# Quarter swaps of convolution weights as transfers, interval products on two row tiles, and norms' roots by Newton steps

## The chip, the cores and the metric

The kernel runs on one core of a Trainium2 chip. The metric is the device time of one execution in microseconds, the median of several runs. TensorE (PE) multiplies matrices, VectorE is DVE, ScalarE is ACT, GpSimd is POOL; SyncE (SP) issues nearly all transfers here. A transfer is issued by a queue in program order, waits there for what it depends on, and lands some time later.

## The reference

The network takes x of shape (4, 32, 32, 16) in float32 through four residual layers, each `x = x + layer(groupnorm(x))` with eight groups of two channels. Layers 0, 1 and 3 are a position-dependent convolution:

```python
first = einsum('ijyx,byxc->bijc', M, inputs)
shifted = conv(inputs, K)      # 3x3, SAME; one kernel per position (i, j): 32*32*16 output channels
diff = relu(inputs - shifted)  # for every (i, j) an image of 32x32x16
second = einsum('ijyx,bijyxc->bijc', W, diff)
return first - second
```

So for each of 1024 positions (i, j), each of 16 channels and each of 4 images there is a whole 32x32 image of the 3x3 convolution (144 products each), then a minimum with zero, a weighting with W and a sum. Layer 2 treats the image's two sides as the ends of intervals: running maxima and minima, two steps of `max over k of sigmoid(f[i,k] Wf + r[k,j] Wr + b)`, and a last product with a sigmoid.

## The kernel before, in words

The four images are two groups of two (`NG`, `GB`). Six phases run one after the other: (group, convolution layer) for three layers. A phase has 8 chunks of 128 positions, a chunk 32 steps (channel f, image b), so there are 1536 steps. A step fills a pair of PSUM banks with 128 positions by 1024 pixels.

The convolution is a product over 144 rows, in float32r[...]. So weights and images are split in a high and a low part. Weights of four channels (`FU`) are a unit, and a unit serves 8 steps; there are 192 units. The first two (`PLAIN`) are used unsplit, in float32. All products use row tiles of 64 partitions: the two halves of the partition range work at once on the two halves of an image. Each half needs the other's weights too, so every split unit `parts` has two slots: slot 0 as computed, slot 1 with its halves of 64 partitions exchanged.

`prep_parts` (L220) is a generator that makes the units. Each step takes one `next` of it, so one unit's turn is spread over 8 steps. In it, `prep` (L208) subtracts the identity from the raw weights of the next unit on POOL; L203 takes the high bits on DVE; ACT scales and copies (L236, L240, L175 in `halve`); POOL subtracts (L237), adds W9 (L238) and WD (L241); then four casts on POOL (L243, L245) exchange quarters of 32 partitions between WU and WL. At last SP issues two transfers that fill slot 1 (L251) and the load of the raw weights two units on (L110 in `load_raw`). `parts` has three buffers, `raw` two.

In a step, `first_part` (L642) issues four pairs of products (ib with WL, ia with WU) and scales the sum on ACT (L663); `second_part` (L666) of the step before issues three pairs (iyz with WD, im9 with W9) and the product and sum on DVE (L680). Matmuls are on line L627.

All other work is laid between the steps by a second generator, `behind` (L733). What it yields is the number of steps to wait; `IDLE` or `CALM` means to wait until the yield of `prep_parts` in that step names this kind. In phase p it makes the inputs of phase p+1: the interval layer where due (L484), the norm (`group_norm`, L312), the copy to `xs` in DRAM and back into `raw` by 8 and 24 transfers (L381, L392), the split of both images (L274) and `place` (L290), which issues 12 transfers in one go. Further, it loads M in eight parts (L414) and issues the first terms (L418). In phase 0 it begins with `rest_of_start` (L869), which splits and places the first two images. W's rows are loaded at step 4 of each chunk (L116).

The schedule is written out by hand: the instructions of an engine and of SP's queue run in program order, and the order of the two generators in a step is: the next of `prep_parts`, the products, then `behind`.

```python
may = next(parts, (IDLE, CALM)) if n or at >= FIRST else (IDLE, CALM)
...
open_steps.append((step, first_part(step)))
if len(open_steps) > 1:
    second_part(*open_steps.pop(0))
wait -= 1
if wait <= 0 and (kind > 0 or kind in may):
    kind = wait = next(behind, 1 << 20)
```

Of the kernel before, what the change touches and what calls it, by code (L numbers as in the profile page):

```python
# [8 lines left out]
F32 = mybir.dt.float32  # L9
# [6 lines left out]
P = 128  # L16
# [28 lines left out]
def net_kernel(ctx: ExitStack, tc: tile.TileContext, x, xq, xi, convs, iv_w, iv_b, out):  # L45
# [162 lines left out]
    def prep(u, at=0, to=FU, eng=nc.gpsimd):  # L208
# [4 lines left out]
        for s in range(2 if u < PLAIN else 1):  # L213
# [3 lines left out]
                ALU.subtract,  # L217
            )

    def prep_parts():  # L220

        for u in range(PLAIN, n_chunks * NU):
            parts = wpool.tile([P, 2, 3, FU, P], F32R, tag="parts", bufs=AHEAD + 1, name=f"parts_{u}")
            W9 = wpool.tile([P, FU, P], F32R, tag="W9", bufs=AHEAD + 1, name=f"W9_{u}")
            units[u] = [parts[:, :, k] for k in range(3)] + [W9]
            src = raws.pop(u)
            w8 = src[:, 0].rearrange("p f k -> p (f k)")  # L230
            WU, WL, WD = (parts[:, 0, k].rearrange("p f k -> p (f k)") for k in range(3))
            high = upper(src[:, 0:1], 1, f"w{u}")[:, 0]
            yield (IDLE,)
            halve(W9, src[:, 1], low_w)
            yield ()
            nc.scalar.activation(WD, high, AF.Copy, scale=-EPS)  # L236
            nc.gpsimd.tensor_tensor(WL, w8, high, ALU.subtract)  # L237
            nc.gpsimd.tensor_tensor(W9, W9.bitcast(F32), src[:, 2], ALU.add)  # L238
            yield ()
            nc.scalar.copy(WU, high)  # L240
            nc.gpsimd.tensor_tensor(WD, WD.bitcast(F32), WL.bitcast(F32), ALU.add)  # L241
            for lo, hi in QUARTERS:
                nc.gpsimd.tensor_copy(WU[hi], WL[lo].bitcast(F32))  # L243
            for lo, hi in QUARTERS:
                nc.gpsimd.tensor_copy(WL[lo], high[hi])  # L245
            yield ()
            prep(u + 1)
            yield (IDLE,)
            yield (IDLE, CALM)
            for h in range(2):  # L250
                nc.sync.dma_start(  # L251
                    parts[64 * h : 64 * h + 64, 1].bitcast(F32),
                    parts[64 - 64 * h : 128 - 64 * h, 0].bitcast(F32),
                )
            load_raw(u + RAWS)
            yield (IDLE, CALM)
            yield (IDLE, CALM)

    def prep_plain(u, at=0, to=FU, eng=nc.gpsimd):
        if at == 0:  # L260
# [48 lines left out]
    def pair_view(ap):  # L309
        return ap.rearrange("p t (g s) -> p t g s", s=2)  # L310

    def group_norm(g, name, dst, gap):  # L312


        def sums(src):
            nc.vector.tensor_reduce(
                part[:, : GC // 2], src.rearrange("p t (g s) -> p g t s", s=2), axis=AX.XY, op=ALU.add
            )

        def totals(name):  # L320

            turned = work.tile([P, 32], F32, tag="turned", name=f"turned_{name}")
            nc.vector.transpose(turned, part)
            by_quarter = work.tile([32, 4], F32, tag="by_quarter", name=f"by_quarter_{name}")
            for q in range(4):
                nc.vector.tensor_reduce(
                    by_quarter[:, q : q + 1], turned[32 * q : 32 * q + 32], axis=AX.X, op=ALU.add
                )
            yield gap
            total = work.tile([P, 32], F32, tag="total", name=f"total_{name}")  # L330
            for q in range(4):
                nc.vector.tensor_reduce(
                    total[32 * q : 32 * q + 32, 0:1], by_quarter, axis=AX.X, op=ALU.add
                )
            yield gap
            whole = work.tile([P, 32], F32, tag="whole", name=f"whole_{name}")
            nc.vector.transpose(whole, total[:, 0:1].to_broadcast([P, 32]))
            return whole[:, : GC // 2]

        sums(X[g])  # L340
        yield gap
        m = yield from totals(f"m{name}")
        mean = work.tile([P, GC // 2], F32, tag="mean", name=f"mean_{name}")
        nc.gpsimd.tensor_scalar_mul(mean, m, 1.0 / (2 * NP))
        xc = work.tile([P, NT, GC], F32, tag="xc", name=f"xc_{name}")
        nc.gpsimd.tensor_tensor(pair_view(xc), pair_view(X[g]), spread(mean), ALU.subtract)
        sq = work.tile([P, NT, GC], F32, tag="sq", name=f"sq_{name}")
        nc.gpsimd.tensor_tensor(sq, xc, xc, ALU.mult)
        yield 4
        sums(sq)  # L350
        yield gap
        yield IDLE
        nc.scalar.activation(spare, spare, AF.Sqrt)
        v = yield from totals(f"v{name}")
        yield 2
        yield IDLE
        rstd = work.tile([P, GC // 2], F32, tag="rstd", name=f"rstd_{name}")
        nc.scalar.activation(rstd, v, AF.Sqrt, bias=eps, scale=1.0 / (2 * NP))
        yield 2
        nc.vector.reciprocal(rstd, rstd)  # L360
        nc.gpsimd.tensor_tensor(pair_view(dst), pair_view(xc), spread(rstd), ALU.mult)
        yield 3

# [54 lines left out]
    def first_terms(layer, mt):  # L418


        sums = bank_pair(f"pf_{layer}")
        for g in range(NG):
            for pt in range(NT):
                for j in range(4):
                    nc.tensor.matmul(  # L425
                        sums[32 * j : 32 * j + 32, g, :256],
                        lhsT=xns[g][:, pt, :], rhs=mt[:, pt, j, :],
                        start=pt == 0, stop=pt == NT - 1, tile_position=(0, 32 * j),
                    )
        ft = work.tile([P, NG, NT * GC], F32, tag="fs", name=f"ft_{layer}")  # L430
        for g in range(NG):
            nc.vector.transpose(ft[:, g], sums[:, g, : NT * GC])
        yield 1
        for g in range(NG):
            nc.vector.tensor_tensor(
                X[g], X[g], ft[:, g].rearrange("p (t m) -> p t m", t=NT), ALU.add
            )
            yield 1
# [7 lines left out]
    def constants():  # L446
        nc.sync.dma_start(wv, iv_w)
        nc.sync.dma_start(bv, iv_b)
        mask2 = const.tile([P, GB], F32, name="mask2")
        nc.vector.tensor_reduce(  # L450
            mask2, ident.rearrange("p (s b c) -> p b s c", b=GB, c=C), axis=AX.XY, op=ALU.add
        )

        nc.gpsimd.tensor_scalar_mul(mask2[GC : 2 * GC], mask2[GC : 2 * GC], -1.0)
        yield 2

        def blocks(dst, k, mask, n, p0=0):
            p = dst.shape[0]
            nc.gpsimd.tensor_tensor(
                dst,  # L460
                wv[p0 : p0 + p, k, :].unsqueeze(1).to_broadcast([p, n, C]),
                mask[p0 : p0 + p].unsqueeze(2).to_broadcast([p, n, C]),
                ALU.mult,
            )

        nc.gpsimd.memset(rt, 0.0)
        yield 1


        for k, hidden, name in ((0, None, "f0"), (3, 2, "f1"), (6, 5, "f2")):  # L470
            n = 64 if hidden is None else 96
            t = const.tile([n, GB, C], F32, name=name)
            blocks(t[:64], k, mask2, GB)
            if hidden is not None:
                blocks(t[64:], hidden, mask2, GB, 64)
            iv[name] = t.rearrange("p k c -> p (k c)")
            yield 1
        for k, name in ((1, "r0"), (4, "r1")):
            t = const.tile([64, NQ * GB, C], F32, name=name)
            for q in range(NQ):  # L480
                blocks(t[:, q * GB : (q + 1) * GB, :], k, mask2, GB)
            iv[name] = t.rearrange("p k c -> p (k c)")
            yield 1
    def interval_layer(g):  # L484
# [37 lines left out]
        def running(dst, src):  # L522
# [16 lines left out]
            out=r[:R, :H, 1:], in_=table(one), pattern=[[-1, H], [1, H]], compare_op=ALU.is_ge,  # L539
            fill=0.0, base=0, channel_multiplier=0,  # L540
        )
        yield 5

        def left(name, wf):
# [9 lines left out]

        def right_side(name, wr):

            for k0 in range(0, T1, 11):
                j0 = k0 + 1
                ps = bank(f"ps_{name}{g}{k0}")
                n = T1 - j0  # L560
                nc.tensor.matmul(  # L561
                    ps[:, : 11 * n], lhsT=wr, rhs=r[:R, k0 : k0 + 11, j0:], start=True, stop=True
                )
                nc.scalar.copy(
                    rt[:, j0:, k0 : k0 + 11],
                    ps[:, : 11 * n].rearrange("p (k j) -> p j k", j=n),
                )
                yield 1

        def step(name, ftp, bias):  # L570
# [17 lines left out]
                last = t  # L588
                yield 6 if i < QI else 3
            yield IDLE  # L590
            nc.scalar.activation(spare, spare, AF.Sigmoid)
            yield 2
            yield IDLE
            nc.scalar.activation(s, s, AF.Sigmoid, bias=bias)
# [224 lines left out]
    nc.vector.tensor_copy(mean_own, ps[:, :1])  # L819
    nc.vector.tensor_scalar_sub(XQ, XQ, mean_own)  # L820
    s2 = const.tile([P, 1], F32, name="s2")
    squares = const.tile([P, 256], F32, name="squares")
    nc.vector.scalar_tensor_tensor(
        squares, XQ, 1.0, XQ, op0=ALU.mult, op1=ALU.mult, accum_out=s2
    )
# [154 lines left out]
```

## Time and profile before

| | |
|---|---|
| median of three runs | 2477.75 us (2477.5 to 2477.88) |
| the profiled execution | 2478.41 us, of which the span is 2476.7 us |
| granted clock of TensorE | 1.000 |
| PE busy | 2458.2 us, 99% of the span |
| DVE, ACT, POOL busy | 2087.3, 1878.4, 1579.7 us (84%, 76%, 64%) |
| transfers | 366.92 MB; SP's queue 53.0% of the 16 DMA engines' span |
| POOL's casts between quarters | 380 + 380, 231.1 + 231.6 us |
| ACT's table loads | five of 1283 ns |

The page gives one line for each group of instructions: line, engine, operation, output and inputs, shapes, count, then busy time in us, the mean of one in ns, and the idle time of the engine just before with what ended it. The lines on transfers give the count, the KB of one and the median us from issue to landing. The chain is followed back from the last instruction to what released it, and gives shares of the span.

### The profile page before, as it was taken

Reading aid. Unit: us, or ns where it says so; the run is one execution under the profiler, and the core shown is the slowest. Engines: PE = TensorE matmul, PEld = TensorE weight load, DVE = VectorE, ACT = ScalarE, POOL = GpSimd, SP = SyncE. Lnnn points to the kernel's source line nnn. Section 1 sums busy time; section 2 is a strip of 40 time slices with the busy share of each in tenths; the row PEclk is TensorE's granted clock in tenths of the full one; section 3 lists DMA queues with packets and bytes.
Section 4 is the critical chain, followed back from the end, with each engine's and each line's share of the span. In section 5 each row is a group of like instructions: output and inputs, shape, how many; then the busy total and the mean of one; then the engine's idle time right before and its main releaser. Section 6 shows DMA issues by size and latency. Waiting matters only on the chain.

```text
span 2476.7 us, 58058 instructions
## 1 busy us (share of the span) xinstructions
PE 2458.2 (99%) x21906; PEld 2090.1 (84%) x21906; DVE 2087.3 (84%) x3617; ACT 1878.4 (76%) x2181; POOL 1579.7 (64%) x1750
## 2 busy tenths in 40 slices
PE   8999999999999999999999999999999999999999
PEld 5999888888888888888888988888998888888887
DVE  9888878888888888778898988899889888788887
ACT  4778767787777778777777777787777787677776
POOL 4766655666565657555567777586878676555552
PEclk9999999999999999999999999999999999999999
DMA  6446754466454467644454545574455467554442
GB/s 198 138 137 182 203 155 135 124 182 164 133 143 135 135 168 198 186 116 134 136 145 127 142 124 140 146 196 125 126 138 144 127 181 195 154 148 137 137 137 54
DMA packets 97673, 366.92 MB, mean 148 GB/s; under 512 B 26480, under 2 KB 31472, under 8 KB 97392
## 3 DMA queue, kind: packets, MB, share of 16 engines
q1 hardware_dynamic: 96832, 362.79, 53.0%
q8 instruction: 172, 2.82, 0.5%
q14 instruction: 109, 0.89, 0.1%
q10 hardware_dynamic: 432, 0.39, 0.1%
q0 software_dynamic: 128, 0.02, 0.0%
HBM read 199.78 MB, written 1.02 MB: 81 GB/s over the span
## 4 chain that ended last, share of the span: by engine, by line
PE 94%; DVE 2%; issue 1%; DMA 1%; ACT 0%; SPq 0%; POOL 0%; ACTq 0%; DVEq 0%; POOLq 0%
PE pc L627 93%; DVE junk L680 1%; PE pf L425 1%; DMA raw<-in_g 1%; ACT pc L663 0%; DMA first<-in_g 0%; SPq L298 0%; DVE raw L846 0%; SPq L300 0%; PE ps_l L548 0%; PE ps_r L561 0%; DMA parts<-parts 0%; DVE tables L508 0%; DVE raw L854 0%; DMA ib<-first 0%
## 5 line engine op out<-in xcount | busy, mean ns | idle before, releaser
L680 DVE SCALAR_TENSOR_TENSOR junk<-pc,WT 128x1024 f32<-128x1024 f32 x1536 | 1879.5, 1224 | 359.1 <-PE pc L627 308.3
L663 ACT ACTIVATE pc<-pc 128x1024 f32<-128x1024 f32 x1520 | 1532.0, 1008 | 561.0 <-PE pc L627 535.8
L627 PE MATMUL pc<-ib,parts 64*128 64x512 f32 x6080 | 958.5, 388 | 4.1 <-DVE junk L680 3.4
L627 PE MATMUL pc<-iyz,parts 64*128 64x512 f32 x6080 | 955.5, 387 | 2.2 <-ACT pc L663 2.0
L627 PE MATMUL pc<-ia,parts 64*128 64x496 f32 x6080 | 933.5, 379 | 0.0
L627 PEld LDWEIGHTS pc<-ia,parts 64*128 64x128 f32 x6080 | 595.5, 184 | 100.8
L627 PEld LDWEIGHTS pc<-ib,parts 64*128 64x128 f32 x6080 | 591.5, 184 | 105.0 <-DVE junk L680 9.9
L627 PEld LDWEIGHTS pc<-iyz,parts 64*128 64x128 f32 x6080 | 592.5, 184 | 88.4 <-ACT pc L663 6.4
L627 PE MATMUL pc<-im,W 64*128 64x496 f32 x3072 | 611.5, 384 | 0.0
L237 POOL TENSOR_TENSOR parts<-raw,upper_w 128x512 fp32r<-128x512 f32 x190 | 248.5, 1308 | 500.2 <-DVE upper_w L203 434.8
L627 PEld LDWEIGHTS pc<-im,W 64*128 64x128 f32 x3072 | 303.0, 184 | 54.5 <-issue 3.2
L243 POOL CAST parts<-parts 32x512 fp32r<-32x512 f32 x380 | 231.1, 608 | 50.1 <-ACT parts L240 31.8
L238 POOL TENSOR_TENSOR W<-W,raw 128x512 fp32r<-128x512 f32 x190 | 247.6, 1303 | 1.8 <-ACT W L175 1.8
L241 POOL TENSOR_TENSOR parts<-parts 128x512 fp32r<-128x512 f32 x190 | 246.8, 1299 | 2.0 <-ACT parts L236 1.9
L245 POOL CAST parts<-upper_w 32x512 fp32r<-32x512 f32 x380 | 231.6, 609 | 22.8
L214 POOL TENSOR_TENSOR raw<-raw,ident 128x512 f32<-128x512 f32 x190 | 199.9, 1052 | 52.2 <-DMA raw<-in_g 28.7
L175 ACT ACTIVATE W<-raw,low_w 128x512 fp32r<-128x512 f32 x190 | 136.2, 717 | 0.1
L680 DVE DVE_READ_ACCUMULATOR junk<-pc,WT 128x1 f32 x1536 | 127.5, 83 | 0.0
L236 ACT ACTIVATE parts<-upper_w 128x512 fp32r<-128x512 f32 x190 | 118.8, 625 | 6.6 <-DVE upper_w L203 6.4
L240 ACT CAST parts<-upper_w 128x512 fp32r<-128x512 f32 x190 | 116.5, 613 | 0.0
L695 POOL TENSOR_SCALAR acc<-acc 128x32 f32<-128x32 f32 x40 | 16.4, 409 | 141.7 <-DVE junk L680 139.7
L203 DVE TENSOR_SCALAR upper_w<-raw 128x512 int32<-128x512 int32 x190 | 86.1, 453 | 1.2 <-POOL raw L214 0.9
(139 smaller groups left out, 479.4 us busy)
## 6 DMA issues: line engine op xcount, KB each, us to landing
raw<-in_g SPq DMA_DIRECT2D x190, 768.0 KB, 7.1
parts<-parts SPq DMA_DIRECT2D x380, 384.0 KB, 4.9
WT<-in_w SPq DMA_DIRECT2D x48, 512.0 KB, 4.6
MT<-in_mt SPq DMA_DIRECT2D x24, 512.0 KB, 7.4
raw<-xs SPq DMA_DIRECT2D x120, 71.8 KB, 2.9
ib<-temp SPq DMA_DIRECT2D x40, 128.0 KB, 2.6
ia<-temp SPq DMA_DIRECT2D x80, 62.0 KB, 3.4
ib<-first SPq DMA_DIRECT2D x8, 128.0 KB, 2.4
```

Of the source, the lines that this page charges most:

```text
L175: nc.scalar.activation(dst, src, AF.Copy, scale=mask[:, 1:2])
L214: eng.tensor_tensor(raws[u][:, s, at:to], raws[u][:, s, at:to], pick[s][:, f0 + at : f0 + to].unsqueeze(2).to_broadcast([P, to - at, P]), ...
L236: nc.scalar.activation(WD, high, AF.Copy, scale=-EPS)
L237: nc.gpsimd.tensor_tensor(WL, w8, high, ALU.subtract)
L238: nc.gpsimd.tensor_tensor(W9, W9.bitcast(F32), src[:, 2], ALU.add)
L240: nc.scalar.copy(WU, high)
L241: nc.gpsimd.tensor_tensor(WD, WD.bitcast(F32), WL.bitcast(F32), ALU.add)
L243: nc.gpsimd.tensor_copy(WU[hi], WL[lo].bitcast(F32))
L245: nc.gpsimd.tensor_copy(WL[lo], high[hi])
L627: nc.tensor.matmul(ps[:, h, at : at + n], lhsT=w[r], rhs=v[r] if n == NH else v[r][:, :n], start=first and k == 0, stop=k == len(pairs) - ...
L663: nc.scalar.activation(ps, ps, AF.Copy, scale=1.0 + EPS)
L680: nc.vector.scalar_tensor_tensor(junk, ps.rearrange("p h n -> p (h n)"), 0.0, chunks[n], op0=ALU.min, op1=ALU.mult, accum_out=accs[phase][ ...
```

## The change

- The turn of a unit is ordered anew. POOL's subtraction (WL) comes before its sum for W9, and that for WD last. The four casts between quarters go; instead SP issues two transfers WL to WU and later two from the high part to WL. The two transfers that fill slot 1 (`exchange`) are issued in the turn of the next unit. `load_raw` moves ahead of the quarter transfers. The kinds that the yields name change with it, the number of yields per unit stays eight. The high part has two buffers of its own.
- The right products of the interval layer are placed on two row tiles: the pooled table is copied to partitions 64 to 127 (`below`), the weights have both copies, and the three products go to one pair of banks, the first on the upper tile, the other two on the lower.
- The norms' reciprocal roots come from an integer first guess (two operations on DVE) and four Newton steps on POOL (16 small operations) instead of a root on ACT and a reciprocal on DVE. The table of the sigmoid is fetched once, behind the first terms of layer 0.
- `squares` in the start shares the buffer `junk`.

```diff
+    def exchange(parts):
+        if parts is not None:
+            for h in range(2):
+                nc.sync.dma_start(
+                    parts[64 * h : 64 * h + 64, 1].bitcast(F32),
+                    parts[64 - 64 * h : 128 - 64 * h, 0].bitcast(F32),
+                )
+
     def prep_parts():
+        swapped = None
         for u in range(PLAIN, n_chunks * NU):
...
-            high = upper(src[:, 0:1], 1, f"w{u}")[:, 0]
+            halve(W9, src[:, 1], low_w)
+            yield (CALM,)
+            high = work.tile([P, FU * P], F32, tag="high", bufs=2, name=f"high_{u}")
+            nc.vector.tensor_scalar(
+                high.bitcast(I32), w8.bitcast(I32), HIGH, None, op0=ALU.bitwise_and
+            )
+            exchange(swapped)
             yield (IDLE,)
-            halve(W9, src[:, 1], low_w)
-            yield ()
+            prep(u + 1)
             nc.scalar.activation(WD, high, AF.Copy, scale=-EPS)
             nc.gpsimd.tensor_tensor(WL, w8, high, ALU.subtract)
+            yield (CALM,)
+            nc.scalar.copy(WU, high)
             nc.gpsimd.tensor_tensor(W9, W9.bitcast(F32), src[:, 2], ALU.add)
-            yield ()
-            nc.scalar.copy(WU, high)
+            yield (CALM,)
             nc.gpsimd.tensor_tensor(WD, WD.bitcast(F32), WL.bitcast(F32), ALU.add)
-            for lo, hi in QUARTERS:
-                nc.gpsimd.tensor_copy(WU[hi], WL[lo].bitcast(F32))
-            for lo, hi in QUARTERS:
-                nc.gpsimd.tensor_copy(WL[lo], high[hi])
-            yield ()
-            prep(u + 1)
-            yield (IDLE,)
-            yield (IDLE, CALM)
-            for h in range(2):
-                nc.sync.dma_start(
-                    parts[64 * h : 64 * h + 64, 1].bitcast(F32),
-                    parts[64 - 64 * h : 128 - 64 * h, 0].bitcast(F32),
-                )
             load_raw(u + RAWS)
             yield (IDLE, CALM)
+            for lo, hi in QUARTERS:
+                nc.sync.dma_start(WU[hi].bitcast(F32), WL[lo].bitcast(F32))
             yield (IDLE, CALM)
+            yield (IDLE, CALM)
+            for lo, hi in QUARTERS:
+                nc.sync.dma_start(WL[lo].bitcast(F32), high[hi])
+            swapped = parts
+            yield (IDLE, CALM)
+        yield (IDLE, CALM)
+        exchange(swapped)
...
+    def inverse_root(v, name):
+        n = GC // 2
...
+        nc.gpsimd.tensor_scalar(a, v, 1.0 / (2 * NP), 1e-5, op0=ALU.mult, op1=ALU.add)
+        nc.vector.tensor_scalar(
+            t.bitcast(I32), a.bitcast(I32), 1, None, op0=ALU.logical_shift_right
+        )
+        nc.vector.tensor_scalar(
+            y.bitcast(I32), t.bitcast(I32), -1.0, float(0x5F3759DF), op0=ALU.mult, op1=ALU.add
+        )
+        nc.gpsimd.tensor_scalar_mul(a, a, -0.5)
+        for pause in (1, 1, IDLE, 2):
+            yield pause
+            nc.gpsimd.tensor_tensor(t, a, y, ALU.mult)
+            nc.gpsimd.tensor_tensor(t, t, y, ALU.mult)
+            nc.gpsimd.tensor_scalar(t, t, 1.5, None, op0=ALU.add)
+            nc.gpsimd.tensor_tensor(y, y, t, ALU.mult)
+        return y
...
-        nc.scalar.activation(spare, spare, AF.Sqrt)
         v = yield from totals(f"v{name}")
-        yield 2
-        yield IDLE
-        rstd = work.tile([P, GC // 2], F32, tag="rstd", name=f"rstd_{name}")
-        nc.scalar.activation(rstd, v, AF.Sqrt, bias=eps, scale=1.0 / (2 * NP))
-        yield 2
-        nc.vector.reciprocal(rstd, rstd)
+        rstd = yield from inverse_root(v, name)
...
+        if layer == 0:
+            nc.scalar.activation(spare, spare, AF.Sigmoid)
...
+        below = tables[R:, : T1 * T1].rearrange("p (i j) -> p i j", j=T1)
+        nc.gpsimd.tensor_copy(below, r[:R])
+        tops = (r[:R], below)
...
-            for k0 in range(0, T1, 11):
+            ps = bank_pair(f"ps_{name}{g}")
+            blocks = []
+            for k0, h, at in ((0, 0, 0), (11, 1, 0), (22, 1, 11 * (T1 - 12))):
                 j0 = k0 + 1
-                ps = bank(f"ps_{name}{g}{k0}")
                 n = T1 - j0
+                blocks.append((k0, j0, n, ps[:, h, at : at + 11 * n]))
                 nc.tensor.matmul(
-                    ps[:, : 11 * n], lhsT=wr, rhs=r[:R, k0 : k0 + 11, j0:], start=True, stop=True
+                    blocks[-1][3], lhsT=wr[R * h : R * h + R], rhs=tops[h][:, k0 : k0 + 11, j0:],
+                    start=True, stop=True,
                 )
+            for k0, j0, n, sums in blocks:
                 nc.scalar.copy(
...
             yield IDLE
-            nc.scalar.activation(spare, spare, AF.Sigmoid)
             yield 2
...
-    squares = const.tile([P, 256], F32, name="squares")
+    squares = work.tile([P, NP], F32, tag="junk", name="squares")[:, :256]
```

More of the change, by code (lines that the diff above doesn't have):

```diff
@@ L310, in pair_view @@
         return ap.rearrange("p t (g s) -> p t g s", s=2)
+    def inverse_root(v, name):
+        n = GC // 2
+        a, y, t = (
+            work.tile([P, n], F32, tag=tag, name=f"{tag}_{name}") for tag in ("root_a", "root_y", "root_t")
+        )
[5 more added lines that the diff above has]
+            y.bitcast(I32), t.bitcast(I32), -1.0, float(0x5F3759DF), op0=ALU.mult, op1=ALU.add
+        )
+        nc.gpsimd.tensor_scalar_mul(a, a, -0.5)
[6 more added lines that the diff above has]
+        return y
     def group_norm(g, name, dst, gap):
@@ L452, in constants @@
         )
-        nc.gpsimd.tensor_scalar_mul(mask2[GC : 2 * GC], mask2[GC : 2 * GC], -1.0)
+        for at in (GC, 3 * GC):
+            nc.gpsimd.tensor_scalar_mul(mask2[at : at + GC], mask2[at : at + GC], -1.0)
         yield 2
@@ L478, in constants @@
         for k, name in ((1, "r0"), (4, "r1")):
-            t = const.tile([64, NQ * GB, C], F32, name=name)
+            t = const.tile([P, NQ * GB, C], F32, name=name)
             for q in range(NQ):
@@ L555, in right_side @@
         def right_side(name, wr):
-            for k0 in range(0, T1, 11):
+            ps = bank_pair(f"ps_{name}{g}")
+            blocks = []
+            for k0, h, at in ((0, 0, 0), (11, 1, 0), (22, 1, 11 * (T1 - 12))):
                 j0 = k0 + 1
-                ps = bank(f"ps_{name}{g}{k0}")
                 n = T1 - j0
+                blocks.append((k0, j0, n, ps[:, h, at : at + 11 * n]))
                 nc.tensor.matmul(
-                    ps[:, : 11 * n], lhsT=wr, rhs=r[:R, k0 : k0 + 11, j0:], start=True, stop=True
+                    blocks[-1][3], lhsT=wr[R * h : R * h + R], rhs=tops[h][:, k0 : k0 + 11, j0:],
+                    start=True, stop=True,
                 )
+            for k0, j0, n, sums in blocks:
                 nc.scalar.copy(
-                    rt[:, j0:, k0 : k0 + 11],
-                    ps[:, : 11 * n].rearrange("p (k j) -> p j k", j=n),
+                    rt[:, j0:, k0 : k0 + 11], sums.rearrange("p (k j) -> p j k", j=n)
                 )
```

## The prediction, made before the changed kernel ran

> **What bounds the kernel now.** I read the page's shares first, then its chain, then the transfers, then the timeline of SP's queue at the start.
>
> ```profile
> PE 2458.2 (99%) x21906; PEld 2090.1 (84%) x21906; DVE 2087.3 (84%) x3617; ACT 1878.4 (76%) x2181; POOL 1579.7 (64%) x1750
> PE 94%; DVE 2%; issue 1%; DMA 1%; ACT 0%; SPq 0%; POOL 0%; ACTq 0%; DVEq 0%; POOLq 0%
> L243 POOL CAST parts<-parts 32x512 fp32r<-32x512 f32 x380 | 231.1, 608 | 50.1 <-ACT parts L240 31.8
> L245 POOL CAST parts<-upper_w 32x512 fp32r<-32x512 f32 x380 | 231.6, 609 | 22.8
> raw<-in_g SPq DMA_DIRECT2D x190, 768.0 KB, 7.1
> parts<-parts SPq DMA_DIRECT2D x380, 384.0 KB, 4.9
> ia<-temp SPq DMA_DIRECT2D x80, 62.0 KB, 3.4
> ```
>
> TensorE is the bound. A step is seven pairs of row-tiled matmuls, and steps follow at 1.567 us (median distance of the DVE products of L680); 1536 of them are 2407 us of a span of 2476.7. The rest is the start (step 20 gets going at 50.5 us), 3 x 7.1 us of first terms, some 9 us of interval matmuls and about 7.5 us of short stalls. POOL is at 64%: its four casts of 0.61 us per unit are beside the path, since a unit lasts 8 steps = 12.5 us and POOL spends 8.3 us on it. So little can be won; what counts is whether a unit's weights stay ahead of the matmuls.
>
> The start, from SP's timeline (start, length, line, transfer) and PE's:
>
> ```profile
> 24.77 3.33 SPq L298 DMA_DIRECT2D ia<-first  x4
> 28.15 2.03 SPq L300 DMA_DIRECT2D ib<-first  x2
> 30.23 2.50 SPq L298 DMA_DIRECT2D ia<-first  x4
> 32.77 1.29 SPq L300 DMA_DIRECT2D ib<-first  x2
> 34.16 1.19 SPq L251 DMA_DIRECT2D parts<-parts  x2
> 35.39 1.21 SPq L110 DMA_DIRECT2D raw<-in_g  x1
> 36.69 3.33 SPq L298 DMA_DIRECT2D ia<-first  x4
> ...
> 43.33 0.64 PE L627 MATMUL pc<-ib,parts 64*128 64x512 f32 x4
> ```
>
> SP issues in program order: place of image 0 (12 transfers, about 0.63 us each), the half swap of unit 2, the load of unit 4, place of image 1. Unit 2's swap landed at 39.8 and step 16, its first user, began at 43.3. The load issued at 35.39 landed at 45.45, and the four small ones issued behind it at 36.69 to 39.49 landed at 45.6 to 46.2: **what stands behind a load on this queue lands after it**. Also, the eighth transfer after a load is not issued before that load lands (here 45.47 after 45.45; again 1603.96 after 1603.94).
>
> **What the Trainium skill says.** "DMA: Bandwidth & Descriptors", section "Queues, rings and completion order": one SDMA engine takes descriptors in ring order, without a promise of order over all engines; the landings above show the order in practice. Its section "Anatomy of one DMA" (GpSimd's path) has a fixed cost of about 2.0 us; here a 62 KB copy from SBUF to SBUF with nothing ahead landed 2.0 us after issue on SP. "ScalarE: Activation LUTs", section "What ACT_TABLE_LOAD costs": 1283 ns; the trace has five loads of 1283 ns. "TensorEngine Tiling (Array Packing)", section "Key Properties": different tiles may work in parallel; here the two 64-row matmuls of a pair start 3 to 4 ns apart.
>
> **Part 1, the swaps.** Removed: four casts, 2.43 us of POOL per unit, hidden now. Added: four 64 KB transfers per unit and three waits in a row on SP: WU's quarter goes behind load_raw, WL's quarter waits for it to land, and the half swap, now issued in the next unit's turn, waits for that. Behind these waits stand, on SP, the next load of `raw`, WT, MT, and the convolution input's transfers; POOL's `prep` waits for the load, PE for the swap. Before, the swap waited once, for POOL.
>
> The chain per unit, from `high` on DVE = 0: POOL's two adds (1.30 each) free `raw` at 0.45 + 2.60 = 3.05; the load is issued 3.05 to 4.2 and lands at 7.7 (1.9 us before data moves and 2.7 us of data, as 611.09 - 608.41 shows behind a swap); WU's quarters are issued to 5.3 and land behind it, 8.0; WL's are issued 8.0 to 9.1 and land at 10.9; the swap is issued 10.9 to 12.0 and lands 5.6 us after its first issue (602.80 to 608.41), at 16.6. The unit's first matmul comes 14 steps after the step of `high`, at about 20.4. **Margin 3.8 us.** Before: `high` at 608.15, swap issued at 615.34, landed at 620.92, used 15 steps after; the trace's median margin is 8.9 us. So in quiet stretches nothing is lost, but the cushion shrinks by about 5 us, while the least margins before were 0.8 (unit 124), 1.1 (42), 1.2 (3, 157), 1.5 (18) and 2.2 us (74): just where `place` and the loads of `raw` from xs fill SP.
>
> Start. The yields put the half swap of unit 2 in step 12, behind place of image 1 in step 11; before it was in step 9. Place of image 0 ends at 34.1 as now; load of unit 4 issued to 35.3, lands at 40 to 41; WU's quarters behind it, 41; WL's issued 41 to 42.2; place of image 1 then takes 12 x 0.63 = 7.6 us, to 49.8; the swap is issued at 49.8 and lands at 55.4. Step 16 begins there, step 20 four steps (6.3 us) later at 61.5, against 50.5: **+11 us**. Unit 3's chain runs meanwhile and arrives at about 67, when step 24 wants it (67.9).
>
> Later phases. Place (7.6 us) falls between WU's and WL's quarters in phases 1 to 4. 2.7 us of it hides in the wait for the load (5.3 to 8.0), so the swap is 4.9 us late, 1.1 more than the margin; the second place meets a queue with no cushion and the limit of eight in flight (five go, then the load's landing at 24.2 must come, then seven more), so the swap lands at 37.2 where 34.0 is wanted, 3.2 more. About 4.5 us per pair in phases 1 and 2, 5.6 in 3 and 4 (a weight load in between), 7.5 in phase 0 where image 0's place falls between WL's quarters and the swap with only the 2 us landing to hide in: 28 in all. The blocks of 8 xs and 24 raw<-xs issues (0.48 us each, 15 us) fall over two units; spread at two per step, mostly into waits, they cost 1.3 in phases 0 to 2; in phases 3 and 4 they are issued four per step, and a swap stands behind most of them: about 7 each. 18 in all. MT's loads (1.8 us of data each) take 1 in phases 0 and 2. Sum **+47, I take 45**. From below: if the idle gaps hide more, 10; from above, with less slack than I count (the margins that this walk gives for the old order come out up to 2 us too large), 75.
>
> POOL's order (subtraction, W9, then WD) and the reused buffer for `squares` cost nothing: POOL has a third of its time free.
>
> **Part 2, right products.** Three fp32 products of 0.59, 0.39 and 0.19 us (352, 231, 110 columns, two passes each) are 1.17 us of PE, four times. On two row tiles the first runs beside the others: at best 0.58 saved each time, 0.29 if in-order issue lets only half overlap: 1.2 to 2.3 us, **I take 1.7**. The copy of `r` (like L534, 2.2 us) hides in the five steps that follow the select.
>
> **Part 3, roots.** Four table loads in phases 3 and 4 (1420, 1564, 1832, 1976) are each followed by a PE stall of 0.55 us; one load remains, behind the first terms at 339 us, where ACT is idle for 7 us. **-2.2 us.** Added: 18 POOL instructions per norm of about 0.25 us (as L344), 4.5 us, eight times; waits of the same length in steps (1+1+2 plus an idle one for 2+2 plus one). POOL's freed time covers it. DVE loses a reciprocal (0.25) and gains two small operations of about 0.17: nothing. Where DVE's copies and scans meet PE's short stalls can shift: 0, from -4 to +4.
>
> **Sum.** The profiled execution took 2478.4 (span 2476.7 and 1.7 around it), 0.7 over the median 2477.75. 2478.4 + 11 + 45 - 1.7 - 2.2 = 2530.5; against the median, 2530.
>
> **Rivals.** (a) Only the start pays: SP's gaps swallow place and xs, since SP waits anyway. For it: the old order came through with 0.8 us. Against: those margins were what was left of 9, and the new chain starts with 4. 2477.75 + 11 - 4 + (0 to 20) = 2485 to 2505. (b) **Faster**: the quarter transfers don't stay behind the load, so that the chain is some 3 us shorter and POOL's relief makes the weights earlier. It decides if unit 2's swap lands before 43.3, which asks for SP to reach it before image 1's place; the program order speaks against it. Then only the savings are left, 3.9 plus up to half of the 7.5 us of stalls: 2470. (c) The casts' removal is not what the transfers replace one for one: if SP falls behind for good (swap 10.9, load landed 19.3, WU 19.6, WL 22.5 and the next swap: 11.6 us against 12.5), every phase loses more, 2565 and above.
>
> **How the numbers follow.** The forecast 0.63, (a) 0.20, (b) 0.10, (c) 0.07. A measurement of this kernel tells about 0.2% (5 us) from no change; a start that costs 11 less the savings and some luck gives 0.05 for the same. Slower 0.85, same 0.05, faster 0.10. The range 2484 to 2565 leaves out (b) and most of (c); the forecast's own is 2505 to 2565.
>
> **What would show it.** The first `ib` matmul of unit 2 at about 55 instead of 43.3, waiting for parts<-parts; PE waits on parts<-parts of 1 to 7 us near the old 195 to 245, 505 to 570, 905 to 970, 1590 to 1625 and 2000 to 2040 us, each later by what was lost before it; SP's waits of L251 turning from POOL to the quarter transfers; POOL near 47% busy; two table loads. Wrong: step 16 at 43, or no PE wait on parts after 70 us.

## The result and the profile after

The changed kernel took 2627.18 us (median of four runs, 2625.03 to 2634.42) against 2477.82 before: 1.0608 times, 95% interval 1.059 to 1.0626. The direction was as forecast. The size was not: +149 us, where +52 was forecast and +87 was the end of the range. The profiled execution has a span of 2626.3 us, 149.6 more than before.

From the page after, in the order of the lines shown of before: busy times and shares, the granted clock of TensorE in 40 slices, the chain, the costliest POOL group by idle time, and the transfers.

```profile
PE 2523.8 (96%) x21906; PEld 2207.3 (84%) x21906; DVE 2088.0 (80%) x3625; ACT 1875.2 (71%) x2159; POOL 1145.7 (44%) x1137
...
PEclk9999999999999999999999999899999989999999
...
PE 70%; DMA 14%; SPq 5%; DVE 4%; issue 3%; POOL 2%; ACT 1%; DVEq 0%; ACTq 0%; POOLq 0%
...
L214 POOL TENSOR_TENSOR raw<-raw,ident 128x512 f32<-128x512 f32 x190 | 201.1, 1058 | 640.4 <-DMA raw<-in_g 441.5
...
raw<-in_g SPq DMA_DIRECT2D x190, 768.0 KB, 5.2
parts<-parts SPq DMA_DIRECT2D x380, 384.0 KB, 4.9
...
parts<-parts SPq DMA_DIRECT2D x380, 64.0 KB, 4.8
parts<-high SPq DMA_DIRECT2D x380, 64.0 KB, 2.0
```

POOL lost 434 us of work, as meant. But PE's share of the chain fell from 94 to 70%, and transfers and SP's queue have 19% of it. WU's quarters (64 KB, 4.8 us) wait behind the load; WL's (2.0 us) don't. More is moved, 416.82 MB instead of 366.92, but the two transfers that the chain had before did not slow down: the half swap still lands 4.9 us after issue in the median, and the load of `raw` after 5.2 instead of 7.1. PE is busy for 65.6 us more with the same 21906 matmuls, and two of its 40 clock slices fell below nine tenths. The waits of after say what PE and ACT waited for (waiter, released by: us in total, times, longest):

```profile
PEld pc L662 <- DMA parts<-parts: 92.1, 50, 9.0
PE pc L662 <- DMA parts<-parts: 72.3, 47, 8.5
...
ACT parts L250 <- DVE high L244: 34.6, 44, 4.7
PEld pc L662 <- ACT pc L698: 31.3, 61, 1.4
```

The first two were absent before, and they count the same waits on two rows of PE. Before, PE's weight loads waited for ACT 6.4 us in 11 waits.

The start, in the timeline of SP's queue and of PE after:

```profile
34.25 0.53 SPq L110 DMA_DIRECT2D raw<-in_g  x1
34.83 1.19 SPq L260 DMA_DIRECT2D parts<-parts  x2
39.34 1.14 SPq L264 DMA_DIRECT2D parts<-high  x2
40.57 2.45 SPq L309 DMA_DIRECT2D ia<-first  x4
43.07 1.29 SPq L311 DMA_DIRECT2D ib<-first  x2
44.40 2.49 SPq L309 DMA_DIRECT2D ia<-first  x4
46.94 1.29 SPq L311 DMA_DIRECT2D ib<-first  x2
48.27 1.24 SPq L223 DMA_DIRECT2D parts<-parts  x2
```

```profile
43.30 0.40 PE L662 MATMUL pc<-ib,parts 64*128 64x512 f32 x2
52.23 0.79 PE L662 MATMUL pc<-ib,parts 64*128 64x512 f32 x1 [8.54 <-DMA parts<-parts]
54.05 0.79 PE L662 MATMUL pc<-ib,parts 64*128 64x512 f32 x1 [1.02 <-DMA parts<-parts]
54.15 1.51 PE L662 MATMUL pc<-ia,parts 64*128 64x496 f32 x4
```

The half swap is issued behind the twelve transfers of place; its halves land at 52.2 and 54.0 (forecast 55.4), and PE stands for 9.6 us. Then four matmuls take 1.51 us, where four took 0.62 before. The trace's record of the granted clock is at 0.50 from 48.6 to 58.8 us, so it fell while PE still stood.

In a quiet stretch the chain runs as worked out. SP's timeline after, one unit from swap to swap:

```profile
834.72 1.14 SPq L223 DMA_DIRECT2D parts<-parts  x2
839.56 0.33 SPq L110 DMA_DIRECT2D raw<-in_g  x1
840.00 1.18 SPq L260 DMA_DIRECT2D parts<-parts  x2
844.58 1.14 SPq L264 DMA_DIRECT2D parts<-high  x2
847.15 2.18 SPq L223 DMA_DIRECT2D parts<-parts  x2
```

On POOL, the subtraction of the unit whose swap is the first of these:

```profile
824.20 1.30 POOL L251 TENSOR_TENSOR parts<-raw,high 128x512 fp32r<-128x512 f32 x1 [4.24 <-DVE high L244]
```

`high` ended at about 824.2, where the subtraction began; the swap issued at 834.72 landed at 840.22, 16.5 us after `high` began (16.6 forecast). The median margin, from the landing of a swap to its unit's first matmul, is 3.0 us (3.8 forecast).

To place the loss I took, for each of the 190 split units, the time from the last `im9` product before it to its first `ia` product, less the 0.665 us of a unit that doesn't wait. Before, these waits sum to 0.4 us; after, to 95.3, in 33 units:

| place | units | forecast | measured |
|---|---|---|---|
| start | 2 | 11 | 10.8 |
| place, phases 0 to 4 | 17, 18; 42, 43; 74, 75; 125, 126; 157, 158 | 28 | 30.5 |
| copies to xs and back | 14; 38, 39; 70, 71; 123; 155 | 18 | 39.6 |
| loads of M and W | 20, 22, 23, 46, 48, 80, 165, 167 | 1 to 2 | 9.3 |
| others | | 0 | 5.1 |

That leaves 54 us that are no waits for weights.

### The profile page after: what moved, and what is told of

Read it like the earlier page. It is cut to its first block, busy times and chain, and to the rows that moved or that the text cites. A ratio compares the mean times of both kernels' runs of the same rounds, so it can differ in the third digit from the quotient of the medians.

```text
span 2626.3 us, 59027 instructions
## 1 busy us (share of the span) xinstructions
PE 2523.8 (96%) x21906; PEld 2207.3 (84%) x21906; DVE 2088.0 (80%) x3625; ACT 1875.2 (71%) x2159; POOL 1145.7 (44%) x1137
## 2 busy tenths in 40 slices
DMA packets 134159, 416.82 MB, mean 159 GB/s; under 512 B 38640, under 2 KB 43632, under 8 KB 133872
## 4 chain that ended last, share of the span: by engine, by line
PE 70%; DMA 14%; SPq 5%; DVE 4%; issue 3%; POOL 2%; ACT 1%; DVEq 0%; ACTq 0%; POOLq 0%
PE pc L662 69%; DMA parts<-parts 9%; DVE junk L715 2%; DMA raw<-in_g 2%; DMA parts<-high 2%; SPq L419 1%; ACT pc L698 1%; PE pf L452 1%; SPq L309 1%; SPq L264 1%; POOL W L254 1%; SPq L223 1%; POOL parts L251 1%; SPq L311 1%; SPq L408 1%
## 5 line engine op out<-in xcount | busy, mean ns | idle before, releaser
L662 PE MATMUL pc<-ib,parts 64*128 64x512 f32 x6080 | 1041.4, 393 | 80.6 <-DMA parts<-parts 72.3
L662 PE MATMUL pc<-iyz,parts 64*128 64x512 f32 x6080 | 1023.1, 393 | 9.9 <-ACT pc L698 9.0
L662 PE MATMUL pc<-ia,parts 64*128 64x496 f32 x6080 | 1004.3, 384 | 0.0
L662 PEld LDWEIGHTS pc<-ib,parts 64*128 64x128 f32 x6080 | 665.1, 186 | 175.7 <-DMA parts<-parts 92.1
L662 PEld LDWEIGHTS pc<-ia,parts 64*128 64x128 f32 x6080 | 665.8, 187 | 72.6
L662 PE MATMUL pc<-im,W 64*128 64x496 f32 x3072 | 665.8, 387 | 0.0
L251 POOL TENSOR_TENSOR parts<-raw,high 128x512 fp32r<-128x512 f32 x190 | 247.1, 1301 | 383.7 <-DVE high L244 292.1
L254 POOL TENSOR_TENSOR W<-W,raw 128x512 fp32r<-128x512 f32 x190 | 247.2, 1301 | 0.1
L250 ACT ACTIVATE parts<-high 128x512 fp32r<-128x512 f32 x190 | 119.2, 627 | 40.0 <-DVE high L244 34.6
L253 ACT CAST parts<-high 128x512 fp32r<-128x512 f32 x190 | 115.9, 610 | 0.0
L730 POOL TENSOR_SCALAR acc<-acc 128x32 f32<-128x32 f32 x40 | 12.5, 312 | 214.7 <-DVE junk L715 210.1
L244 DVE TENSOR_SCALAR high<-raw 128x512 int32<-128x512 int32 x190 | 94.2, 496 | 0.2
```

The lines of the kernel that those rows point to most:

```text
L244: nc.vector.tensor_scalar(high.bitcast(I32), w8.bitcast(I32), HIGH, None, op0=ALU.bitwise_and)
L662: nc.tensor.matmul(ps[:, h, at : at + n], lhsT=w[r], rhs=v[r] if n == NH else v[r][:, :n], start=first and k == 0, stop=k == len(pairs) - ...
```

## The experiments

**What each part costs.** Theory A: part 1 makes the weights late, and TensorE's clock falls after longer waits. Theory B: the other parts carry a good share. The first kernel is the old one with the new `exchange` and `prep_parts` (and `squares` in `junk`'s buffer):

```diff
...
-            for lo, hi in QUARTERS:
-                nc.gpsimd.tensor_copy(WU[hi], WL[lo].bitcast(F32))
...
+            for lo, hi in QUARTERS:
+                nc.sync.dma_start(WU[hi].bitcast(F32), WL[lo].bitcast(F32))
...
```

> The kernel before with part 1 alone (quarter swaps as transfers, the order of POOL's work, the half swap in the next unit's turn); roots and right products as before. Theory A (the chain of three transfer waits on SP makes the weights late, and TensorE's clock drops to half after the longer waits): all of the 149 us come with it, and the savings of the other parts are missing, 2628 to 2635 us. Theory B (Newton's steps on POOL, or the products on two row tiles, carry a good part): below 2580 us.

Measured: 2626.02 us, ratio 1.0599 (1.0583 to 1.0614). Part 1 is the whole loss. The second has parts 2 and 3, with the old `prep_parts`; against the kernel before:

```diff
...
-        rstd = work.tile([P, GC // 2], F32, tag="rstd", name=f"rstd_{name}")
-        nc.scalar.activation(rstd, v, AF.Sqrt, bias=eps, scale=1.0 / (2 * NP))
...
+        rstd = yield from inverse_root(v, name)
...
```

> The changed kernel with part 1 undone: casts on POOL as before, roots by Newton steps and right products on two row tiles kept. Theory A: 3.9 us less than before (2.2 from table loads, 1.7 from the products), 2474 us, from 2470 to 2478. Theory B: over 2500 us.

Measured: 2483.94 us, ratio 1.0021 (1.0012 to 1.003): slower by 5, where 3.9 were to be saved. By units, the savings are there (0.5 us at each of four units with right products, 0.7 at two without a table load), but units 99, 131, 122 to 126 and 154 to 158 lose more. From the waits of this kernel between 1276 and 1290 us, at unit 99:

```profile
DVE upper_w L203 <- POOL raw L214: 2.0, 1, 2.0
PEld pc L651 <- DVE junk L704: 2.0, 2, 1.2
PE pc L651 <- DVE junk L704: 1.2, 2, 0.7
```

My reading: with the casts kept, Newton's steps stand ahead of `prep` on POOL, which began at 1280.72 behind steps from 1279.59 on; DVE stood 2.0 us for it before it could take the high bits, its products came late, and PE waited for a free bank. To tell whether it was the products, they were put into the old kernel alone:

```diff
...
-                    ps[:, : 11 * n], lhsT=wr, rhs=r[:R, k0 : k0 + 11, j0:], start=True, stop=True
+                    blocks[-1][3], lhsT=wr[R * h : R * h + R], rhs=tops[h][:, k0 : k0 + 11, j0:],
...
```

> The kernel before with the right products on two row tiles alone (casts, roots and tables as before). If Newton's steps on POOL made the kernel without part 1 slower (DVE waited 2 us for POOL's prep behind them), this one is 1 to 2 us faster than before, 2476 to 2478. If the copy of the pooled table or the row tiles made it, it is 3 to 6 us slower.

Measured: 2476.71 us, ratio 0.9992 (0.9983 to 1.0001). So the products don't slow it: it is 1.7 us under the runs of before beside it (2478.4), as expected, though the interval just touches no change. That leaves the roots; alone they were not run.

**What the chain waits for.** First, the half swap of unit 2 alone is issued in its own turn again:

```diff
             swapped = parts
+            if u == PLAIN:
+                exchange(parts)
+                swapped = None
```

> The changed kernel, but the half swap of unit 2 alone is issued in its own turn, right after WL's quarters, so ahead of place of image 1. Theory A: it is issued at about 42 and lands at 47.5 instead of 54.0; step 16 starts then; 7 us less, about 2620 us, a little more if the clock stays up. Theory C (the start is bound by image 1's place anyway, since step 20 waits for it): no more than 3 us less.

Measured: 2623.57 us, ratio 1.0593 (1.0576 to 1.0611). The 3.6 us less are within the intervals, so the time decides neither for 7 us nor for under 3. The trace tells more: unit 2's wait fell from 10.8 to 4.1, but unit 3 now waits 3.0, and each wait is followed by a stretch at half clock. Theory A was right about unit 2 and overlooked that the next unit's chain is behind as well.

Then the load of `raw` is issued behind the quarters:

```diff
-            load_raw(u + RAWS)
...
             swapped = parts
+            load_raw(u + RAWS)
```

> The changed kernel, with the load of raw issued after WL's quarters instead of ahead of WU's. Theory A with the wait behind the load as its main part: WU's quarters land at 4.9 us after high instead of 8, WL's at 8, the load at about 11, and the swap, now behind the load, at about 14.3 instead of 16.6; the margin grows by 2.3 us, most waits of PE under that size go, 2560 to 2595 us. Theory D (SP's time for place and the copies from xs sets the waits, wherever the load stands): within 10 us of 2627.

Measured: 2625.7 us, ratio 1.0598 (1.0582 to 1.0614). It came out on the side of theory D (SP's time for the other transfers sets the waits), with no gain that can be told. The load is then ahead of the swap instead of the quarters; the median margin is 3.4 us for 3.0, not 2.3 more.

Next, one of the chain's three waits on SP is taken out: WU's quarters are cast on POOL again.

```diff
+            for lo, hi in QUARTERS:
+                nc.gpsimd.tensor_copy(WU[hi], WL[lo].bitcast(F32))
             load_raw(u + RAWS)
             yield (IDLE, CALM)
-            for lo, hi in QUARTERS:
-                nc.sync.dma_start(WU[hi].bitcast(F32), WL[lo].bitcast(F32))
```

> The changed kernel, but WU's quarters are cast on POOL again (1.2 us per unit) and only WL's quarters are transfers, so one of the three waits of the chain is gone. Theory A: WL's quarters go at about 5.6 us after high and land at 7.7 to 8.7, the swap lands at 14.3 instead of 16.6 at the latest, and SP has 1.2 us of issues less per unit: waits fall by a half, with the clock 60 to 90 us less, 2540 to 2570. Rival (E4's lesson holds for all of the chain, its length doesn't matter): within 10 us of 2627.

Measured: 2585.89 us, ratio 1.0434 (1.0417 to 1.0451). The median margin rose to 5.9 us and the waits fell from 95 to 65, by a third where a half was expected, so the time missed its range of 2540 to 2570. The length of the chain does count: 41 us of 149 hang on this one wait and its two issues, which this kernel takes out together.

**What stands between the chain's steps.** Copies from xs, two per step in phases 3 and 4 too:

```diff
-            if layer < 2 or row % 2:
-                yield 1
+            yield 1
```

> The changed kernel; the copies raw<-xs of layer 2's phases are given out two per step, as in the other layers, instead of four per step. Theory D (the wait before a unit is the time that SP spends on other transfers between the steps of the chain, less the gaps in which SP waits anyway): PE's waits before units 123 and 155 (12.5 and 11.3 us) fall to about those of units 38 and 39 (5 us), 15 us less, about 22 with the clock, 2605 us. Theory E (the waits come from the amount of work per phase, not from its density): under 5 us less.

Measured: 2633.66 us (one run). Unit 123 waits 8.3 instead of 12.5 and unit 155 7.5 instead of 11.3, but units 126, 127, 158 and 159 now wait 6.6, 4.3, 4.0 and 3.0: the sum stays at 95.8. By the time it is theory E (the amount of work counts, not how densely it is issued); by the waits, the spread copies reach into the units that place comes to and leave them no cushion.

The same transfers and place from POOL's queue:

```diff
...
-                nc.sync.dma_start(
+                nc.gpsimd.dma_start(
                     inner[:, h, r], xt[g][GC * r : GC * (r + 1), :, HW * h : HW * h + WP]
...
```

> The changed kernel; the copies to and from xs and, after the start, place are issued from POOL's queue instead of SP's. Theory D: the chain of SP is left with weights, W and M; waits before units 14, 17, 18, 38 to 43, 70 to 75, 123 to 126 and 154 to 158 are gone (some 72 of 95 us), and TensorE's clock stays up there; what is left is the start (13 us), M and W (10) and the small items: 2500 to 2520 us. Rival: POOL's own time for each issue makes the subtractions late by as much: over 2560 us.

Measured: 2622.51 us, ratio 1.0571 (1.0546 to 1.0597). The rival came true, and the kernel doesn't settle theory D. POOL's timeline there, ahead of unit 14:

```profile
190.96 4.70 POOL L408 DMA_DIRECT2D xs<-xt  x8 [2.92 <-DVE xt L402]
195.67 1.05 POOL L214 TENSOR_TENSOR raw<-raw,ident 128x512 f32<-128x512 f32 x1
196.66 1.30 POOL L251 TENSOR_TENSOR parts<-raw,high 128x512 fp32r<-128x512 f32 x1
197.92 1.30 POOL L254 TENSOR_TENSOR W<-W,raw 128x512 fp32r<-128x512 f32 x1
```

These eight issues cost POOL 0.59 us each, in front of the sum (L254) that frees `raw`. Therefore the transfers were left out altogether:

```diff
-        for r in range(ROWS):
+        for r in range(0):
...
-            for h in range(2):
+            for h in range(0):
                 off = tap // 3 * WP + tap % 3
```

> The changed kernel without the 8 copies to xs and the 24 copies from xs into raw per convolution input (left out: later phases work on the first phase's image). Theory D: the waits before units 14, 15, 38, 39, 70, 71, 123 and 155 (40 us) go, with them some six stretches at half clock (about 2 us each), 50 to 60 us less: 2565 to 2580 us. Theory F (each cycle of the chain is late by itself in these phases, through M's and W's loads or POOL): waits of several us stay there, over 2600 us.

Measured: 2574.12 us, ratio 1.0386 (1.0365 to 1.0407). The waits before 14, 38, 39, 70, 71, 123 and 155 are gone; the sum is 59.1. Without place in later layers as well:

```diff
-            yield from place(g, b, temp)
+            yield from place(g, b, temp) if layer == 0 else (1,)
```

> As before it (no copies to and from xs) and without place in the layers after the first (left out: the split images of later layers; place of phase 0 and of the start stays). Theory D: of the waits, the start (10.8 us), phase 0's place (up to 7.7) and M and W (up to 9) stay; the clock falls to half only around those: 2510 to 2535 us. Theory F: over 2570 us.

Measured: 2532.34 us, ratio 1.0217 (1.0197 to 1.0238). Waits sum to 27.0, of which 10.9 are the start and 7.2 phase 0's place; two stretches at half clock are left of 15. The control is the kernel before with the same transfers left out:

> The kernel before without the same transfers (no copies to and from xs, no place after the first layer): the control. Every theory: nothing of them is on the path there, 2472 to 2479 us.

Measured: 2475.41 us, ratio 0.9987 (0.9978 to 0.9996). The same 32 and 24 transfers per phase cost the old order 3 us and the new one 95. Theory D holds, and theory F (the chain is late by itself) falls: what stands between the chain's steps makes most of the loss. These kernels take away the transfers' bytes together with their place in SP's queue; that it is the place in the queue is read from the timelines and from the swap's median landing time, 4.8 us without them and 4.9 with them.

**What a wait of PE costs.** Eight waits put into the old kernel, one per chunk:

```diff
...
+                if at == 14 and n in HOLDS:
+                    hold_pe(phase, t, steps[at - 2], HOLDS[n])
...
+        for k in range(n):
+            nc.gpsimd.tensor_tensor(hold, ident, ident, ALU.mult)
+        nc.tensor.matmul(
+            bank(f"ps_hold_{phase}_{t}")[:, :1], lhsT=ident, rhs=hold[:, 0:1], start=True, stop=True
+        )
...
```

> The kernel before with eight deliberate waits of PE in quiet chunks of phases 1 and 2: a small product waits for a chain of 0, 2, 4, 6, 8, 11, 14 and 20 POOL operations that starts when DVE ends the sum two steps back. About 0.3 us per operation and 1 to 2 us at the base, so waits of 1 to 8 us. Theory A on the clock: waits under 2 us cost themselves alone; those over about 3.5 us are followed by a stretch of 3.4 us or a multiple at half clock, which costs 1 to 3 us more. Rival (the excess over the waits has another source, such as slower operands while transfers run): each wait costs its own length and the clock record stays at one.

Measured: 2545.46 us (one run). By the clock record and the start of the next unit:

| PE idle, us | 1.87 | 2.83 | 3.77 | 4.82 | 5.69 | 7.12 | 8.55 | 11.40 |
|---|---|---|---|---|---|---|---|---|
| unit later by, us | 2.50 | 5.03 | 7.25 | 8.22 | 8.41 | 9.45 | 11.06 | 14.25 |
| at half clock, us | 0 | 3.4 | 6.8 | 6.8 | 6.8 | 6.8 | 10.2 | 13.7 |

PE's timeline at the third wait:

```profile
713.16 0.58 PE L714 MATMUL ps_hold<-hold,ident 128*128 128x1 f32 x2 [3.77 <-POOL hold L713]
713.68 1.22 PE L627 MATMUL pc<-ib,parts 64*128 64x512 f32 x4
...
718.47 1.06 PE L627 MATMUL pc<-iyz,parts 64*128 64x512 f32 x4
719.32 0.46 PE L627 MATMUL pc<-im,W 64*128 64x496 f32 x2
...
720.53 0.62 PE L627 MATMUL pc<-iyz,parts 64*128 64x512 f32 x4
```

Four products take 1.06 us until 719.3 and 0.62 after 720. The shortest wait costs 0.63 over its idle time with the clock at one, the small product among it. The seven others cost 2.2 us more than idle time and these 0.63 on average (1.6 to 2.9). The rival, slower operands while transfers run, is out: behind the longest wait the clock is at half with no transfer moving (stretch, us, busy time of PE, clock, share and GB/s of transfers):

```profile
1273.00:1277.00 4.00, 2.67 (x12) 0.50 0.00 0
```

## Why the prediction was wrong

**Right.** PE as the bound with nothing to win in quiet stretches; the direction; the order of SP's queue at the start and its 11 us; the chain's 16.6 us and its shrunken margin; place at 28 against 30.5, within 1.6 us in each phase and so not by luck; most of the units that would wait; the products on row tiles, as far as 1.7 us can be told. Its list of least margins left out units 156 and 125 (1.4 and 1.8 us), of which only 125 came to wait, 1.4 us.

**The step that failed most: a wait was priced at its length, and the clock at nothing.** The sum put 56 us of waits (11 and 45) down as 56 us of time. After has 15 stretches at half clock, 88.7 us in all. They stand at exactly the 15 units whose wait, by the measure of the table, is 2.1 us or more; the 18 others, up to 1.9 us, have none. Step by step against before, and without the waits, the steps that touch these stretches take 28 us more, 1.5 to 3.0 per stretch; the deliberate waits, at 2.2 us each, would give 33. The windows view around unit 14 gives, from left to right, the stretch and its length in us, the busy time with its count of PE, PEld, DVE, ACT and POOL, the granted clock, and share and GB/s of transfers:

```profile
207.00:212.00 5.00, 3.02 (x22) 1.79 (x18) 2.72 (x6) 1.87 (x2) 4.28 (x4) 1.00 0.48 121
212.00:216.00 4.00, 0.79 (x1) 0.28 (x1) 0.00 (x0) 0.00 (x0) 0.00 (x0) 0.55 0.95 220
216.00:220.00 4.00, 3.74 (x20) 3.07 (x22) 0.76 (x1) 1.73 (x2) 0.00 (x0) 0.59 0.86 255
```

PE is nearly idle from 212 to 216, and from 216 to 220 it works at 0.59 of its clock. The Trainium skill has this on "TensorE: Matmul & The Clock Gate", section "What's actually happening": a free-running window of about 3.4 us decides on half or full clock, and an idle one brings half. The stretches here are multiples of 3.4 us, which agrees. That the idle time must fill a window does not: a deliberate wait of 2.83 us sufficed, and at unit 75 a wait of 2.1 us, in which PE also worked in between. Nor is the length a sharp rule: waits of 3.7 us in the kernel without the xs copies (unit 43) and of 3.8 us in the one with POOL's queue (unit 156) had no stretch at half clock. In the profile of before all 40 slices of the clock are at 9, so nothing there warned of it; the prediction has no term for it.

**Mis-sized: the copies to and from xs**, 39.6 us where 18 were worked out. SP's timeline ahead of unit 14 shows four things that the walk lacked:

```profile
188.86 1.14 SPq L223 DMA_DIRECT2D parts<-parts  x2
190.47 6.60 SPq L408 DMA_DIRECT2D xs<-xt  x8
197.12 0.45 SPq L116 DMA_DIRECT2D WT<-in_w  x1
197.92 1.20 SPq L419 DMA_DIRECT2D raw<-xs  x2
199.17 0.42 SPq L110 DMA_DIRECT2D raw<-in_g  x1
199.63 0.91 SPq L419 DMA_DIRECT2D raw<-xs  x2
200.63 1.18 SPq L260 DMA_DIRECT2D parts<-parts  x2
202.38 4.35 SPq L419 DMA_DIRECT2D raw<-xs  x4
207.17 1.15 SPq L264 DMA_DIRECT2D parts<-high  x2
208.37 1.98 SPq L419 DMA_DIRECT2D raw<-xs  x4
210.45 1.14 SPq L223 DMA_DIRECT2D parts<-parts  x2
```

The eight issues take 6.6 us and not the 3.8 of 0.48 each. The second copy back then waits for the last landing in DRAM (198.74), and the load of `raw`, free to go when POOL's sum ends at 191.6, stands behind it until 199.17. W's half megabyte is ahead of the load, which lands 7.2 us after issue; in the quiet stretch it was 4.8. And the last of the four copies of 202.38 is the eighth transfer behind that load: it goes out at 206.43, when the load has landed (206.41). The prediction had seen this limit and counted it for place, but not here. From swap to swap it takes 21.6 us instead of 12.5. The walk let these copies fall mostly into SP's gaps. In truth they open gaps of their own, and everything behind waits. Before's trace could have warned: in phase 3 the same issues, 8 and then 12 of 24, took 5.3 and 9.9 us, where 0.48 each gives 3.8 and 5.8:

```profile
1581.78 5.26 SPq L381 DMA_DIRECT2D xs<-xt  x8
...
1596.24 9.90 SPq L392 DMA_DIRECT2D raw<-xs  x12
```

**Missing: some 20 us that are neither waits for weights nor clock.** In the same comparison, 22 us lie in steps away from every wait and stretch: 13 of them in units that differ by less than 0.4 us each, the rest in single units, mostly of the two phases that make the interval layer. The kernel without copies and place still has 20 us of this kind, and the one with part 1 alone has 27, so they come with part 1 and not with its late swaps. One source is seen in the traces and was not tried by itself: `high` now comes one step closer, on DVE, to ACT's scaling of it. ACT stood 34.6 us for it (6.4 before, in five waits), and PE's weight loads stood 31 us for ACT.

**Wrong sign: parts 2 and 3 together**, -3.9 forecast, +5.1 measured with the casts kept. The savings were sized nearly rightly (2.0 us on the products where 1.7 were forecast, 1.4 on the tables where 2.2 were); "POOL's freed time covers it" can hold only where part 1 has freed POOL. In the full change they made no difference that can be told (2626.0 without, 2627.2 with them).

The sum: 95 us of waits, 28 of half clock, 5 in the steps at and just behind the shorter waits, and 22 elsewhere make the 149.6 to within 1 us. Against the forecast that is 39 us more of waits, 22 of them at the xs copies; 28 for the clock; 27 of small items; and 4 of savings that did not show. How the small items divide stays open.

## What to carry to other kernels

A work-saving transfer that takes its place in a chain on an in-order queue is priced by what else stands on that queue between its steps, at the places with the least margin, and not by its own length. Find those places in the profile before, as the time from landing to first use, and charge each wait of TensorE that can exceed some 2 us with the clock as well, about 2 us each here. Freeing an engine that was not the bound brought nothing by itself.

## What was not expected of the hardware

Deliberate waits of PE of 2.83 us and more brought 3.4 to 13.7 us at half clock, at a cost of 1.6 to 2.9 us over the wait; 1.87 us did not. In the changed kernel the waits of 2.1 us and more did, those up to 1.9 us did not. Eight small transfers to DRAM took 0.44 to 1.70 us each to issue while a swap of 2 x 384 KB was on its way.
